# Where layer 0 puts the routing arithmetic and the projections of the next head pair

## The chip, the cores and the metric

The kernel runs on one core of one Trainium2 chip. The metric is the device time of one execution in microseconds; the times shown are medians of several runs. The profile shows one execution, engine by engine: TensorE (PE, with PEld for its weight loads), VectorE (DVE), ScalarE (ACT), GpSimd (POOL) and SyncE (SP).

## The reference, cut to what matters

The input `x` has eight images of 256 channels and 32 x 32 places, taken as 1024 tokens of 256. Layer 0 is attention with 8 heads of 64; its softmax runs over the queries (axis 1 of `i, j`), not over the keys:

```python
qkv = (xt @ w_qkv + b_qkv).reshape(B, S, N_HEADS, 3 * D_K)
attn = jnp.einsum('bihd,bjhd->bijh', q, k) * SCALE
attn = jax.nn.softmax(attn, axis=1)
res = jnp.einsum('bijh,bjhd->bihd', attn, v).reshape(B, S, N_HEADS * D_K)
res = res @ w_out + b_out + xt
```

Layer 1 normalises the tokens and adds a one-head attention over them; then it normalises again and adds a mixture of eight experts, of which each token uses two:

```python
logits = tokens @ router_w.T
probs = jax.nn.softmax(logits, axis=-1)
rw, re = jax.lax.top_k(probs, TOP_K)
rw = rw / jnp.maximum(rw.sum(-1, keepdims=True), 1e-12)
out = out + combine[:, e:e + 1] * y      # y: expert e's two-layer network
```

Everything is in float32.

## The kernel before, in words

The images are worked on one after another. For each image come layer 0 (`layer0`, line 370), the attention of layer 1 (`attend`, line 549) and the normalisation with the router's logits (`normed`, line 715). Seven images then send their normalised tokens to a table in HBM, sorted by expert; the experts run over that table afterwards, and the eighth image goes through the experts without sorting.

Layer 0 goes through the 8 heads in 4 pairs. A pair `g` has 8 steps `j`, one for each block of 128 keys, so a step is named (g, j) here, and `at` counts the 32 steps through. In a step both heads of the pair get their scores `psc` (line 395), as matmuls on 64 x 64 quarters of TensorE; a head's 1024 scores per key lie in a PSUM buffer called `big`, of which there are three. VectorE takes the maximum of the first half (`first_max`, line 410) and of the second half (line 422); ScalarE takes the exponential of the whole and its sum (line 432), which frees the buffer. VectorE turns the sum into its reciprocal and scales the values with it (`divide`, lines 441 and 443). Two steps later (`LAG = 2`) the value products `po` (`gather_values`, line 463) use the exponentials, in two turns of four matmuls. They add up over the 8 steps of a pair in two PSUM buffers; after the pair's last step ScalarE copies both to `res` (line 482), and only then can the next pair's products begin in the same buffers. Products that write the same half are kept apart by an empty instruction on SP (on POOL for image 0), which each turn waits for (line 471).

The queries and keys of pair g + 1 are made while pair g runs: `project` (line 294) is four matmuls of 128 x 512 into one more `big` buffer (line 300) and two evictions by VectorE (line 290). In the kernel before, the queries are projected in step (g, 3) and the keys in (g, 5), for g = 0, 1, 2.

The routing of the image before is fed into the layer 0 of the image after it. `dispatch` (line 728) and `gates` (line 641) are generators: each `yield` ends a portion, and layer 0 runs one portion in each step (lines 509 and 520). A portion is a few operations on 128 x 64 or 128 x 8 elements on VectorE, placed by `issue_after` behind the step's second first-half maximum. The portions are: softmax over the experts, the best and the second-best expert, their gates, two small matmuls `pcn` that count tokens before this one (lines 743 and 744), a running sum, the row of the table for each token and choice, and then 16 scatters on POOL, each preceded by a cast of its row numbers to integers on VectorE (line 795) and each one indirect DMA (line 797). Image 0 has no routing beside it.

The order in which an engine executes is fixed when the program is built: a scheduler places the instructions of each engine in the order of the program text, its priorities (`issue_after` among them) and the buffers, so matmuls of neighbouring calls can stand interleaved.

Of the kernel before, what the change touches and what calls it, by code (L numbers as in the profile page):

```python
# [11 lines left out]
I32 = mybir.dt.int32  # L12
# [7 lines left out]
def kernel(  # L20
# [349 lines left out]
    def layer0(b, xT, begun, routing):  # L370
# [8 lines left out]
        res = one.tile([P, NPAIR, S], F32, tag="res", name=f"res_{b}")  # L379
        steps = [(g, j) for g in range(NPAIR) for j in range(NT)]  # L380
        LAG = 2
        seconds, turned = {}, {}

        relay = nc.gpsimd if b == 0 else nc.sync
# [98 lines left out]
            return mm  # L483

        last = len(steps) - 1
        for at in range(last + LAG + 1):
            if at <= last:
                score(at, 0, 0)
            if 0 < at <= last + 1:
                score(at - 1, 1, 1)  # L490
                soften(at - 1, 1)
            if at >= LAG:
                gather_values(at - LAG, 0)
            if at <= last:
# [12 lines left out]
            if at == 0:  # L507
                begun.rest()
                next(routing, None)
            if at >= LAG:  # L510
                array = gather_values(at - LAG, 1)
            if at <= last:
                g, j = steps[at]
                if g + 1 < NPAIR and j in (3, 5):
                    if j == 3:
                        qks.append([])
                    qks[g + 1].append(project(b, xT, g + 1, len(qks[g + 1])))
                if array is not None:
                    with tc.issue_after(firsts[at, 1].ins), tc.issue_after(array.ins):
                        next(routing, None)  # L520
        for _ in routing:
            pass

# [117 lines left out]
    def gates(b, lT):  # L641


        def tmp(tag):
            return small.tile([P, NT, E], F32, tag=tag, name=f"{tag}_{b}", bufs=1)

        def col(tag):
            return small.tile([P, NT], F32, tag=tag, name=f"{tag}_{b}", bufs=1)

        n = S // NG  # L650
        pt = acc(f"plT_{b}")
        for j in range(n // P):
            nc.tensor.transpose(pt[:, ts(j, P)], lT[:, ts(j, P)], ident)

        l = tmp("g_l")
        nc.vector.tensor_copy(
            l.rearrange("p (g j) e -> p j g e", g=NG),
            pt[:, :n].rearrange("p (j g e) -> p j g e", g=NG, e=GC)[:, :, :, :E],
        )
        yield  # L660
        m = col("g_m")
        nc.vector.tensor_reduce(m, l, AX.X, ALU.max)
        p = tmp("g_p")
        nc.vector.tensor_sub(p, l, bcast(m, E))
        nc.scalar.activation(p, p, AF.Exp)
        yield
        z = col("g_z")
        nc.vector.tensor_reduce(z, p, AX.X, ALU.add)
        nc.vector.reciprocal(z, z)
        nc.vector.tensor_mul(p, p, bcast(z, E))  # L670
        yield

        def first_of_max(src, tag):
            top, best = col(f"{tag}_top"), col(f"{tag}_best")
            hot = tmp(f"{tag}_hot")
            nc.vector.tensor_reduce(top, src, AX.X, ALU.max)
            nc.vector.tensor_tensor(hot, src, bcast(top, E), ALU.is_equal)
            yield
            nc.vector.tensor_mul(hot, hot, rank)
            nc.vector.tensor_reduce(best, hot, AX.X, ALU.max)  # L680
            nc.vector.tensor_tensor(hot, hot, bcast(best, E), ALU.is_equal)
            return top, hot

        top1, hot1 = yield from first_of_max(p, "g_1")
        yield
        rest = tmp("g_rest")
        nc.vector.scalar_tensor_tensor(rest, hot1, -2.0, p, ALU.mult, ALU.add)
        top2, hot2 = yield from first_of_max(rest, "g_2")
        yield
        total = col("g_total")  # L690
        nc.vector.tensor_add(total, top1, top2)
        nc.vector.tensor_scalar_max(total, total, 1e-12)
        nc.vector.reciprocal(total, total)
        gate = keep.tile([P, 2, NT], F32, tag="gate", name=f"gate_{b}")
        nc.vector.tensor_mul(gate[:, 0], top1, total)
        nc.vector.tensor_mul(gate[:, 1], top2, total)
        return gate, (hot1, hot2)
# [30 lines left out]
    def dispatch(b, n2, l, group):  # L728

        gate, hots = yield from gates(b, l)  # L730
        yield

        def tmp(tag):
            return small.tile([P, NT, E], F32, tag=tag, name=f"{tag}_{b}", bufs=1)


        both = tmp("d_both")
        nc.vector.tensor_add(both, hots[0], hots[1])
        yield
# [7 lines left out]
        yield  # L747
# [11 lines left out]
        yield  # L759
# [12 lines left out]

        kept = []
        tos = []
        for k in range(2):
            yield
# [8 lines left out]
            yield  # L785
            to = small.tile([P, NT], F32, tag="d_to", name=f"d_to_{b}_{k}", bufs=2)
            nc.vector.scalar_tensor_tensor(to, exp, float(group.cap), row, ALU.mult, ALU.add)
            kept.append((row, exp))
            tos.append(to)
            group.kept[b] = gate, kept  # L790

        for k in range(2):
            for i in range(NT):
                at = small.tile([P, 1], I32, tag="d_at", name=f"d_at_{b}_{i}_{k}", bufs=4)
                nc.vector.tensor_copy(at, tos[k][:, i : i + 1])  # L795
                view = group.views[2 * (NT * group.items.index(b) + i) + k]
                nc.gpsimd.indirect_dma_start(  # L797
                    out=view[:, :],
                    out_offset=bass.IndirectOffsetOnAxis(ap=at, axis=0),
                    in_=n2[:, i, :],  # L800
                    in_offset=None,
                )
                yield

    def plan(group):

# [371 lines left out]
    begun = Begin(0, next_x)  # L1178
    begun.all()
    prepare()  # L1180
    routing = iter(())
    for b in range(B):
        xT = next_x
        if b + 1 < B:
# [65 lines left out]
```

## Time and profile before

| | |
|---|---|
| median of 3 runs | 2530.41 us (2528.81 to 2532.02) |
| profiled execution | 2521.92 us |
| its span in the profile | 2520.2 us |
| TensorE busy | 2421.3 us (96%) |
| VectorE busy | 1565.1 us (62%) |
| ScalarE busy | 887.7 us (35%) |
| GpSimd busy | 386.4 us (15%) |
| layer 0 of image 2, from 549.05 to 687.50 us | 138.45 us: TensorE busy 133.90, VectorE 112.54, ScalarE 77.45 |

In a line of the timeline the first number is the start in us from the span's beginning, the second the duration; then follow the engine, the line of the kernel, the operation, the tiles written and read, and how many instructions were merged. A bracket at the end gives the idle time of the engine just before and what ended it. One matmul of the kernel shows as two instructions[...]; hence groups of eight for four matmuls. Busy times of TensorE are modelled and overlap where quarters of the array run beside each other.

### The profile page before, as it was taken

The numbers are of one execution on the slowest core, as the hardware profiler recorded it, in microseconds if no ns is written. First come the engines' busy times: TensorE is split into PE (matmuls) and PEld (weight loads), VectorE is DVE, ScalarE is ACT, GpSimd is POOL, SyncE is SP. The second block draws the span as 40 slices with busy tenths as digits, with TensorE's granted clock in tenths as the row PEclk, the third lists the DMA queues.
The fourth block names the chain that finished last, engine by engine and source line by source line (L and its number), as shares of the span: only waits on it lengthen the run. The fifth ranks groups of instructions, "written<-read, shape, count | busy, mean of one in ns | idle before, by whom it ended". The sixth has DMA issues, their size and how long they took to land.

```text
span 2520.2 us, 37152 instructions
## 1 busy us (share of the span) xinstructions
PE 2421.3 (96%) x14015; PEld 1334.8 (53%) x14015; DVE 1565.1 (62%) x3836; ACT 887.7 (35%) x1491; POOL 386.4 (15%) x383
## 2 busy tenths in 40 slices
PE   9999999999999999999999999999999999997799
PEld 3356434653465346533663356335633688875466
DVE  5774677468755884578557855875578643334443
ACT  2541355125512561246225521552154422211222
POOL 0000002000200020002000100010001344434452
PEclk9999999999999999999999999999999999998899
DMA  7992001000100000000000000000001266653353
GB/s 281 385 361 69 34 3 44 6 17 1 35 17 17 1 30 21 17 1 28 24 17 1 25 27 17 1 22 14 1 18 49 91 214 213 217 186 101 98 162 119
DMA packets 82556, 188.23 MB, mean 75 GB/s; under 512 B 13992, under 2 KB 23880, under 8 KB 80584
## 3 DMA queue, kind: packets, MB, share of 16 engines
q1 hardware_dynamic: 57368, 118.65, 13.1%
q0 software_dynamic: 25008, 67.20, 8.6%
q8 instruction: 111, 1.82, 0.3%
q14 instruction: 69, 0.57, 0.1%
HBM read 100.49 MB, written 110.90 MB: 84 GB/s over the span
## 4 chain that ended last, share of the span: by engine, by line
PE 72%; DVE 9%; ACT 3%; issue 2%; DMA 1%; another core or an unknown queue 1%; ACTq 0%; DVEq 0%; SPq 0%; POOLq 0%
PE po L463 13%; PE psc L395 12%; PE pqk L300 8%; PE py L602 7%; PE ps L576 6%; PE pr L542 4%; PE ph L937 4%; PE pe L962 3%; PE pv L336 3%; DVE scrap L422 3%; PE pdy L1144 2%; PE pdh L1120 2%; PE px L561 2%; PE pa L595 2%; ACT ex L432 2%
## 5 line engine op out<-in xcount | busy, mean ns | idle before, releaser
L432 ACT ACTIVATE ex<-psc,nmax 128x1024 f32<-128x1024 f32 x512 | 571.1, 1115 | 528.2 <-DVE scrap L422 408.9
L463 PE MATMUL po<-ex,vs 64*64 64x512 f32 x4096 | 612.8, 593 | 25.4 <-ACT res L482 21.3
L395 PE MATMUL psc<-qk,qk 64*64 64x512 f32 x4096 | 613.4, 596 | 17.3 <-ACT ex L432 16.3
L422 DVE TENSOR_SCALAR_CACHE_REDUCE scrap<-psc,nmax 128x512 f32<-128x512 f32 x512 | 383.9, 750 | 118.3 <-PE psc L395 98.7
L410 DVE TENSOR_REDUCE nmax<-psc 128x1 f32<-128x512 f32 x512 | 350.5, 684 | 11.9 <-PE psc L395 11.9
L395 PEld LDWEIGHTS psc<-qk,qk 64*64 64x64 f32 x4096 | 188.0, 132 | 320.7 <-issue 167.8
L463 PEld LDWEIGHTS po<-ex,vs 64*64 64x64 f32 x4096 | 187.2, 132 | 285.0 <-issue 91.3
L602 PE MATMUL py<-n,aT 128*128 128x256 f32 x1024 | 243.5, 392 | 19.3 <-DVE aT L597 14.5
L797 POOL DMA_INDIRECT rows<-n,d_at x112 | 109.3, 976 | 926.1 <-DVE d_at L795 919.7
L602 PEld LDWEIGHTS py<-n,aT 128*128 128x128 f32 x1024 | 195.4, 195 | 84.2 <-DVE aT L597 52.3
L576 PE MATMUL ps<-nT,xa 128*128 128x512 f32 x512 | 236.5, 592 | 0.0
L300 PE MATMUL pqk<-xT,wqkv 128*128 128x512 f32 x512 | 235.0, 602 | 0.1
L587 ACT ACTIVATE ex<-ps,nmax 128x1024 f32<-128x1024 f32 x64 | 71.3, 1115 | 353.7 <-DVE nmax L584 338.5
L607 DVE SCALAR_TENSOR_TENSOR t<-py,rs,t 128x256 f32<-128x256 f32 x64 | 31.0, 484 | 234.3 <-PE py L602 202.3
L723 POOL TENSOR_TENSOR t<-t,n 128x2048 f32<-128x2048 f32 x8 | 36.3, 4533 | 901.6 <-issue 631.3
L300 PEld LDWEIGHTS pqk<-xT,wqkv 128*128 128x128 f32 x512 | 93.3, 190 | 133.0 <-issue 92.8
L576 PEld LDWEIGHTS ps<-nT,xa 128*128 128x128 f32 x512 | 93.6, 190 | 79.9 <-issue 73.6
L1009 POOL DMA_INDIRECT yk<-y,yat x112 | 112.6, 1006 | 122.4 <-DVE o L1041 71.5
L290 DVE TENSOR_SCALAR qk<-pqk,b_qk 128x512 f32<-128x512 f32 x100 | 75.1, 751 | 85.1 <-PE pqk L300 85.1
L336 PE MATMUL pv<-wqkv,xT 128*128 128x512 f32 x256 | 119.6, 597 | 0.8 <-ACT wqkv L106 0.8
L584 DVE TENSOR_REDUCE nmax<-ps 128x1 f32<-128x1024 f32 x64 | 78.3, 1223 | 59.1 <-PE ps L576 58.6
L542 PE MATMUL pr<-wo,res 128*128 128x256 f32 x512 | 111.8, 379 | 0.0
(191 smaller groups left out, 2441.4 us busy)
## 6 DMA issues: line engine op xcount, KB each, us to landing
rows<-wb SPq DMA_DIRECT2D x7, 8192.0 KB
y<-yb SPq DMA_DIRECT2D x63, 256.0 KB
xT<-in_x_dram SPq DMA_DIRECT2D x7, 1024.0 KB
sums<-t SPq DMA_DIRECT2D x7, 1024.0 KB
o<-sums SPq DMA_DIRECT2D x7, 1024.0 KB
out_dram<-oT SPq DMA_DIRECT2D x14, 512.0 KB
wpack<-in_L_ffn_w_dram SPq DMA_DIRECT2D x4, 1024.0 KB
wb<-in_L_ffn_w_dram SPq DMA_DIRECT2D x16, 256.0 KB
```

What stands on the lines that cost most here:

```text
L300: mm = nc.tensor.matmul(pq[:, ts(n, 512)], wqkv[:, cc, t, ts(g, P)], xT[:, cc, ts(n, 512)], start=(cc == 0), stop=(cc == NCC - 1),)
L336: nc.tensor.matmul(pv, self.xT[:, cc, ts(i, P)], wqkv[:, cc, 2, :], start=(cc == 0), stop=(cc == NCC - 1),)
L395: mm = nc.tensor.matmul(pss[at, h][ts(c, DK), ts(n, 512)], k[r, j * P + c * DK : j * P + (c + 1) * DK], q[r, ts(n, 512)], start=True, stop ...
L410: firsts[at, h] = nc.vector.tensor_reduce(nmax, pss[at, h][:, ts(0, 512)], AX.X, ALU.max, negate=True)
L422: seconds[h] = nc.vector.tensor_scalar(scrap, ps[:, ts(1, 512)], -1.0, nmaxes.pop((at, h)), ALU.mult, ALU.min, accum_out=nmax,)
L432: nc.scalar.activation(ex, ps, AF.Exp, bias=nmax, scale=1.0, accum_out=sums[at][:, h : h + 1])
L463: mm = nc.tensor.matmul(po[n][ts(h, DK), :], vss[at][keys, h, :], exps[at, h][keys, ts(n, 512)], start=(j == 0 and turn == 0), stop=(j == ...
L542: nc.tensor.matmul(pr[:, :C], res[:, g, ts(i, P)], wo[:, g, :], start=(g == 0), stop=(g == NPAIR - 1))
L576: nc.tensor.matmul(psc[:, ts(n, 512)], xa[:, ec, ts(i, P)], nT[:, ec, ts(n, 512)], start=(ec == 0), stop=(ec == NCC - 1),)
L602: nc.tensor.matmul(py[:, :D], aT[:, ts(m, P)], n1[:, m, :], start=(m == 0), stop=(m == NT - 1))
L797: nc.gpsimd.indirect_dma_start(out=view[:, :], out_offset=bass.IndirectOffsetOnAxis(ap=at, axis=0), in_=n2[:, i, :], in_offset=None,)
L1009: nc.gpsimd.indirect_dma_start(out=yk[:, i, k, :], out_offset=None, in_=self.group.y[:, :], in_offset=bass.IndirectOffsetOnAxis(ap=ats[k][ ...
```

## The change

Three things move, and one operation is merged; what is computed stays the same.

The steps that project become (0, 3), (0, 5), (1, 1), (1, 5), (2, 1), (2, 5). In step (g, 1) the value products of the pair before end, so there the projection now stands directly behind them.

The routing has fewer `yield`s. Its arithmetic runs in step (0, 0) and beside the first four projections, each portion placed before the projection; the scatters follow from (1, 6) on, one per step. Each scatter gets a dependency on the step's second first-half maximum (`behind`), passed in with `send`. The row numbers are cast once for each choice, 8 columns at a time, in place of once for each scatter.

Where a pair's first value products have no projection in front of them (only in step (3, 2)), their first turn is moved behind the step's remaining scores (`late`).

```diff
+        PROJECT = [(0, 3), (0, 5)]
+        PROJECT += [(g, j) for g in range(1, NPAIR - 1) for j in (1, 5)]
+        FIRST_SCATTER = PROJECT[3]
...
+        def share(behind=None):
+
+            try:
+                routing.send(behind)
+            except StopIteration:
+                pass
+
         for at in range(last + LAG + 1):
+            g, j = steps[min(at, last)]
+
+            late = at > LAG and steps[at - LAG][1] == 0 and (g, j - 1) not in PROJECT
             if at <= last:
                 score(at, 0, 0)
             if 0 < at <= last + 1:
                 score(at - 1, 1, 1)
                 soften(at - 1, 1)
-            if at >= LAG:
+            if at >= LAG and not late:
                 gather_values(at - LAG, 0)
...
             if at == 0:
                 begun.rest()
-                next(routing, None)
+                share()
+            if late:
+                gather_values(at - LAG, 0)
             if at >= LAG:
                 array = gather_values(at - LAG, 1)
-            if at <= last:
-                g, j = steps[at]
-                if g + 1 < NPAIR and j in (3, 5):
-                    if j == 3:
-                        qks.append([])
-                    qks[g + 1].append(project(b, xT, g + 1, len(qks[g + 1])))
-                if array is not None:
-                    with tc.issue_after(firsts[at, 1].ins), tc.issue_after(array.ins):
-                        next(routing, None)
+            project_now = at <= last and (g, j) in PROJECT
+            if at <= last and (project_now or (g, j) > FIRST_SCATTER):
+                with tc.issue_after(firsts[at, 1].ins), tc.issue_after(array.ins):
+                    share(firsts[at, 1])
+            if project_now:
+                if len(qks) == g + 1:
+                    qks.append([])
+                qks[g + 1].append(project(b, xT, g + 1, len(qks[g + 1])))
...
-            tos.append(to)
-            group.kept[b] = gate, kept
+            at = small.tile([P, NT], I32, tag=f"d_at{k}", name=f"d_at{k}_{b}", bufs=1)
+            nc.vector.tensor_copy(at, to)
+            ats.append(at)
+        group.kept[b] = gate, kept
 
         for k in range(2):
             for i in range(NT):
-                at = small.tile([P, 1], I32, tag="d_at", name=f"d_at_{b}_{i}_{k}", bufs=4)
-                nc.vector.tensor_copy(at, tos[k][:, i : i + 1])
+                behind = yield
                 view = group.views[2 * (NT * group.items.index(b) + i) + k]
-                nc.gpsimd.indirect_dma_start(
+                scatter = nc.gpsimd.indirect_dma_start(
                     out=view[:, :],
-                    out_offset=bass.IndirectOffsetOnAxis(ap=at, axis=0),
+                    out_offset=bass.IndirectOffsetOnAxis(ap=ats[k][:, i : i + 1], axis=0),
                     in_=n2[:, i, :],
                     in_offset=None,
                 )
-                yield
+                if behind is not None:
+                    tc.add_manual_dep(scatter.ins, behind.ins.name, BEHIND)
```

The rest of the diff removes `yield`s from `gates` and `dispatch` and turns `first_of_max` into a plain function.

More of the change, by code (lines that the diff above doesn't have):

```diff
@@ L670, in gates @@
         nc.vector.tensor_mul(p, p, bcast(z, E))
-        yield
         def first_of_max(src, tag):
@@ L677, in first_of_max @@
             nc.vector.tensor_tensor(hot, src, bcast(top, E), ALU.is_equal)
-            yield
             nc.vector.tensor_mul(hot, hot, rank)
@@ L682, in first_of_max @@
             return top, hot
-        top1, hot1 = yield from first_of_max(p, "g_1")
-        yield
+        top1, hot1 = first_of_max(p, "g_1")
         rest = tmp("g_rest")
         nc.vector.scalar_tensor_tensor(rest, hot1, -2.0, p, ALU.mult, ALU.add)
-        top2, hot2 = yield from first_of_max(rest, "g_2")
         yield
+        top2, hot2 = first_of_max(rest, "g_2")
         total = col("g_total")
@@ L730, in dispatch @@
         gate, hots = yield from gates(b, l)
-        yield
         def tmp(tag):
@@ L738, in dispatch @@
         nc.vector.tensor_add(both, hots[0], hots[1])
-        yield
         yield
@@ L746, in dispatch @@
         nc.vector.tensor_copy(cn.rearrange("p t i e -> p (t i e)"), pcn[:, : 2 * NT * E])
-        yield
         per = small.tile([P, E, NT], F32, tag="d_per", name=f"d_per_{b}", bufs=1)
@@ L758, in dispatch @@
         )
-        yield
         rows = tmp("d_rows")
@@ L773, in dispatch @@
         kept = []
-        tos = []
+        ats = []
+        yield
         for k in range(2):
-            yield
             hot = hots[k]
@@ L784, in dispatch @@
             nc.vector.tensor_reduce(exp, sel, AX.X, ALU.add)
-            yield
             to = small.tile([P, NT], F32, tag="d_to", name=f"d_to_{b}_{k}", bufs=2)
@@ L802, in dispatch @@
                 )
-                yield
+                if behind is not None:
+                    tc.add_manual_dep(scatter.ins, behind.ins.name, BEHIND)
     def plan(group):
@@ L1180 @@
     prepare()
-    routing = iter(())
+    routing = (nothing(_) for _ in ())
     for b in range(B):
```

## The prediction

> **What bounds the kernel.** I read the page first: TensorE is the path.
>
> ```profile
> span 2520.2 us, 37152 instructions
> ...
> PE 2421.3 (96%) x14015; PEld 1334.8 (53%) x14015; DVE 1565.1 (62%) x3836; ACT 887.7 (35%) x1491; POOL 386.4 (15%) x383
> ...
> PE 72%; DVE 9%; ACT 3%; issue 2%; DMA 1%; another core or an unknown queue 1%; ACTq 0%; DVEq 0%; SPq 0%; POOLq 0%
> ```
>
> So only what keeps TensorE waiting or thinly fed in layer 0, the stage the change touches, can be won. Next, the timeline of image 2, one undisturbed step (start, duration, what):
>
> ```profile
> 682.79 1.22 PE L395 MATMUL psc<-qk,qk 64*64 64x512 f32 x8
> 683.00 1.11 ACT L432 ACTIVATE ex<-psc,nmax 128x1024 f32<-128x1024 f32 x1 [0.32 <-DVE rs L441]
> 683.65 1.22 PE L463 MATMUL po<-ex,vs 64*64 64x512 f32 x8
> 684.01 0.19 ACT L432 ACTIVATION_READ_ACCUMULATOR ex<-psc,nmax 128x1 f32 x1
> ...
> 684.51 1.22 PE L395 MATMUL psc<-qk,qk 64*64 64x512 f32 x8
> ...
> 685.37 1.22 PE L463 MATMUL po<-ex,vs 64*64 64x512 f32 x8
> ```
>
> Four groups of eight follow each other every 0.86 us: a full step is 3.43 us, and VectorE waits for TensorE in it. This is the floor. A pair's switch is not at it:
>
> ```profile
> 665.51 1.06 ACT L482 COPY res<-po 128x512 f32<-128x512 f32 x2
> ...
> 666.14 1.14 PE L463 MATMUL po<-ex,vs 64*64 64x512 f32 x6 [0.90 <-ACT res L482]
> ...
> 668.12 0.75 DVE L422 TENSOR_SCALAR_CACHE_REDUCE scrap<-psc,nmax 128x512 f32<-128x512 f32 x1 [1.32 <-PE psc L395]
> ```
>
> The new pair's value products wait for the copies that free `po`; the scores behind them wait too, so VectorE idles. A step that projects (line 300), last:
>
> ```profile
> 559.34 3.70 PE L300 MATMUL pqk<-xT,wqkv 128*128 128x512 f32 x8
> ...
> 559.78 0.68 DVE L410 TENSOR_REDUCE nmax<-psc 128x1 f32<-128x512 f32 x1
> ...
> 560.38 0.21 DVE L668 TENSOR_REDUCE g_z<-g_p 128x8 f32<-128x64 f32 x1
> ...
> 563.08 0.75 DVE L290 TENSOR_SCALAR qk<-pqk,b_qk 128x512 f32<-128x512 f32 x1 [0.97 <-PE pqk L300]
> ...
> 564.13 0.75 DVE L422 TENSOR_SCALAR_CACHE_REDUCE scrap<-psc,nmax 128x512 f32<-128x512 f32 x1 [0.30 <-PE psc L395]
> ...
> 566.00 0.19 ACT L432 ACTIVATION_READ_ACCUMULATOR ex<-psc,nmax 128x1 f32 x1
> ...
> 566.46 1.04 PE L395 MATMUL psc<-qk,qk 64*64 64x512 f32 x8
> ```
>
> Here VectorE has a hole: between its maximum (done 560.46) and the next reduction (564.13) lie 3.67 us, of which two evictions need 1.50. Cover: 2.17 us.
>
> As a clock I take the starts of line 441's reciprocal, one per step. Plain steps give 3.43, projecting ones 7.23. Pair sums (8, 8, 8 and 7 gaps): image 0, which has no routing, 35.01, 36.67, 36.65, 25.51; image 2, which has it, 36.33, 38.87, 36.66, 25.36. Images 3 to 6 equal image 2 within 0.2. Images 1 and 7 have 6.3 and 5.6 more in one pair (image 1's value products are issued late; the blocks are planned in image 7's), in an order the change leaves alone.
>
> [...] ready scores stand behind the 0.90 us wait. [...] a projection among the 64x64 groups takes 3.63 us on the chain, in the attention part 3.43. [...] 64 elements take 225 ns (line 670), 504 take 676 (line 838), so the 39 small routing operations are nearly all fixed cost. [...] 24 waits for `po`'s two buffers, 21.3 us.
>
> **A, the pair switch (8 images).** In image 0, pair 1 starts 4.58, 3.68, 7.45 where 3.43, 3.43, 7.23 would be plain: 1.62 lost; pair 2: 1.61; pair 3: 4.57, 3.69, 3.47, 1.44 lost. For pairs 1 and 2 the projection now stands behind the last values: 3.63 us of matmuls cover the copies (they end at 666.57, 2.4 us after the last values' group at 664.20), and ScalarE has 4.2 us of idle in a projecting step, so the exponential that the copies delay today is not late. The evictions move with the projection (twice 0.75 us, the same hole in VectorE's row), and the `qk` buffer that they write had its last reader, the scores of the pair before, one step earlier. The whole 3.23 goes; were the projection not long enough, up to 1.6 per switch would come back. For pair 3 eight scores are moved ahead of the first value products. Half of them need the PSUM buffer of the current step's first exponential, whose accumulator read ends 1.41 us after the last values, so they finish about 2.0 after; the copies end at 1.9 to 2.4. Then 16 value products (1.72) and a relay wait (0.1 to 0.3, the trace's end of layer 0) give a step of 3.9 to 4.2, so 0.5 to 0.75 stays; I take 0.70, saving 0.74. Sum 3.97 x 8 = **31.8 us**.
>
> **B, routing out of plain steps (7 images).** A step with three or four small operations becomes VectorE-bound (3.8 to 4.05 us). Image 2 less image 0: pair 0 1.32, pair 1 2.20 (0.91 of it the step that also holds the `pcn` products). 3.52 x 7 = **24.6 us**. The 98 saved casts (143 ns) count nothing: VectorE waited 0.16 us per step even with them.
>
> **C, what comes back (7 images).** The built order puts 9, 11, 7 and 12 small operations into (0,3), (0,5), (1,1), (1,5), ahead of the evictions or among them. Dependent ones start 0.25 us apart (617.00, 617.25, 617.50), the 8-wide ones 0.18: 2.25, 2.4, 1.7, 2.75 us against 2.17. Overrun 0.1, 0.25, none, 0.6. Behind them stand the evictions, then the second head's reduction and exponential, for whose PSUM TensorE's scores wait; slack there is 566.46 - 566.19 = 0.27. Stall: 0, 0, 0, 0.3. In (0,0) two more operations stand before a reduction with 0.45 us of wait: nothing.
> In (1,1) `pcn` now stands *before* the projection and takes the buffer freed by the previous exponential; the projection gets the next one, freed by the current step's first exponential, 1.41 us after the last values plus 0.06 to 0.4 of signalling, where a plain projection starts after 0.14. Stall 1.33 to 1.67, `pcn`'s 0.6 inside; I take 1.5. TensorE's other work queues behind it. (1.5 + 0.3) x 7 = **12.6 us**.
> The 16 scatters, one indirect DMA of 0.97 us on POOL each, move from pair 2's second step to the end of layer 0 into (1,6) to (3,5), behind a maximum each: POOL is idle there; they end earlier, each holding only later scatters and the next image's addition (line 723) behind it, and what waits for them (next normalisation, the experts' gathers) waits no longer than now. SP's queue is unchanged.
>
> Sum: 31.8 + 24.6 - 12.6 = 43.8. The profiled execution took 2521.92 us (span 2520.2): 2478.1; the median of the runs is 2530.41, 0.34% higher, so **2486 us**.
>
> **Rivals.**
> 1. Crowding takes a good part back (2504): small operations at 0.35 us. Then 9, 11 and 12 of them take 3.15, 3.85 and 4.2 us, less cover and slack of 2.44: stalls of 0.7, 1.4 and 1.8 where I have 0.3, so 3.6 x 7 = 25 at most; the eight-wide ones are shorter, I take 18. A stall of 4 us in (1,1) gives the same. For it: three steps already exceed the cover. Against: the 0.25 us is measured in this very queue.
> 2. Stalls only move (2530, within 5): what follows a switch is then bound by ScalarE or VectorE. Against: steady steps show VectorE waiting for TensorE (0.16 us), ScalarE at 0.7 idle.
> 3. Slower (2541): one mechanism, VectorE's queue in steps (0,3), (0,5), (1,5). Their 32 small operations must cost the 43.8 / 7 = 6.3 us gained per image and 0.2 of slack left over: 32 x (s - 0.25) > 6.5, so it decides from a spacing s of 0.45 us; at 0.5 it gives 32 x 0.25 - 0.2 = 7.8 per image, 2541. For it: these operations stand ahead of everything that feeds the next step. Nothing in the trace shows above 0.26.
> That the order is not as described is excluded by the instruction order of both builds.
>
> **Numbers.** Forecast 0.77, rival 1 0.15, rival 2 0.05, rival 3 0.03. Own range of the forecast 2477 to 2496 (pair 3 saving 0 to 1.2, (1,1) 1.3 to 2.5, switches 2.6 to 3.3 per image); with rival 1, 2477 to 2510. A measurement of this kernel tells about 0.2% (5 us) from no change: faster 0.93, same 0.04, slower 0.03.
>
> **What would show it.** A right: no wait of `po` for `res` left but about 8 short ones at pair 3; pair 1 and 2 start with 3.43-like gaps. B right: images 2 to 6 pair 0 at 35.0, VectorE's steps free of small operations. C right: a wait of `pqk` for `ex`, about 1 us, seven times, and pair 1 at 36.8 against image 0's 35.0. Wrong if small operations run slower beside evictions, if POOL's or SP's relays delay the products put back to back in pair 3, or if a fuller TensorE is granted a lower clock.

## The result and the profile after

The changed kernel takes 2485.19 us (median, 2483.84 to 2486.23), the kernel before 2530.69 beside it: a ratio of 0.982, 95% interval 0.9803 to 0.9837. The forecast was 2486. The profiled execution took 2485.58 us, 36.3 less than that of before.

First the page's summary lines, the answer to those of before:

```profile
span 2483.9 us, 37112 instructions
...
PE 2405.0 (97%) x14015; PEld 1310.7 (53%) x14015; DVE 1564.7 (63%) x3738; ACT 888.4 (36%) x1491; POOL 388.6 (16%) x383
...
PE 78%; DVE 4%; ACT 2%; issue 1%; another core or an unknown queue 1%; DMA 1%; ACTq 0%; POOL 0%; DVEq 0%; SPq 0%; POOLq 0%
```

VectorE's busy time is nearly the same (1565.1 before) although 98 instructions are gone, yet its part of the chain that ends last fell from 9% to 4% and TensorE's rose from 72% to 78%: the work was hardly made less, it was moved off the path. Next three of the page's costliest groups, before and after (us busy, mean ns of one, then the idle us of the engine ahead of them and what ended most of it):

```profile
L463 PE MATMUL po<-ex,vs 64*64 64x512 f32 x4096 | 612.8, 593 | 25.4 <-ACT res L482 21.3
L395 PE MATMUL psc<-qk,qk 64*64 64x512 f32 x4096 | 613.4, 596 | 17.3 <-ACT ex L432 16.3
...
L300 PE MATMUL pqk<-xT,wqkv 128*128 128x512 f32 x512 | 235.0, 602 | 0.1
```


```profile
L399 PE MATMUL psc<-qk,qk 64*64 64x512 f32 x4096 | 568.2, 593 | 7.3 <-ACT ex L436 7.2
L467 PE MATMUL po<-ex,vs 64*64 64x512 f32 x4096 | 558.4, 591 | 5.4 <-DVE vs L447 4.1
...
L300 PE MATMUL pqk<-xT,wqkv 128*128 128x512 f32 x512 | 235.0, 602 | 5.4 <-ACT ex L436 5.2
```

The wait of `po` for `res` is gone as a group (21.3 us before), and a new wait of `pqk` for `ex`, 5.2 us, has come. Those are two of the three signs that the prediction named.

The clock of the prediction, the starts of the reciprocal (now line 445), gives the third. Sums in us for image 2, and what the prediction's parts give for the same pair:

| pair | before | after | saved | forecast |
|---|---|---|---|---|
| 0 | 36.33 | 35.08 | 1.25 | 1.32 |
| 1 | 38.87 | 36.41 | 2.46 | 1.62 + 2.20 - 1.5 - 0.3 = 2.02 |
| 2 | 36.66 | 35.05 | 1.61 | 1.61 |
| 3 | 25.36 | 24.98 | 0.38 | 0.74 |
| all | 137.22 | 131.52 | 5.70 | 5.69 |

Over the eight images these sums went from 1106.57 to 1062.38 us: 44.2 saved, 43.8 forecast. Image by image the two lie further apart: image 0 saved 3.57 of 3.97, images 1 to 6 saved 5.42 to 5.83 of 5.69, and image 7 saved 6.76, since its pair 2, beside which the experts' blocks are planned, went from 42.28 to 39.34, 2.94 less where 1.61 was forecast. Behind the last image's layer 0, where the change does nothing, the profiled execution of before took 541.7 us and that of after 549.7; so the two profiled executions differ by 36.3 us only, where the medians differ by 45.5.

Now the three places, from the timeline of image 2 (start, duration, what). The switch to pair 2:

```profile
613.30 1.04 PE L467 MATMUL po<-ex,vs 64*64 64x512 f32 x8
...
614.27 3.70 PE L300 MATMUL pqk<-xT,wqkv 128*128 128x512 f32 x8
...
615.47 1.06 ACT L486 COPY res<-po 128x512 f32<-128x512 f32 x2
...
617.90 1.09 PE L399 MATMUL psc<-qk,qk 64*64 64x512 f32 x8
...
618.81 1.04 PE L467 MATMUL po<-ex,vs 64*64 64x512 f32 x8
```

The copies end at 616.53, 2.3 us before the new pair's value products want `po`. No product waits for them. A step that projects and carries nine routing operations:

```profile
550.01 0.68 DVE L414 TENSOR_REDUCE nmax<-psc 128x1 f32<-128x512 f32 x1
550.61 0.21 DVE L682 TENSOR_REDUCE g_z<-g_p 128x8 f32<-128x64 f32 x1
550.86 0.20 DVE L683 RECIPROCAL g_z<-g_z 128x8 f32<-128x8 f32 x1
...
552.63 0.22 DVE L698 SCALAR_TENSOR_TENSOR g_rest<-g_hot,g_p 128x64 f32<-128x64 f32 x1
552.78 1.40 DVE L290 TENSOR_SCALAR qk<-pqk,b_qk 128x512 f32<-128x512 f32 x2
554.46 0.75 DVE L426 TENSOR_SCALAR_CACHE_REDUCE scrap<-psc,nmax 128x512 f32<-128x512 f32 x1 [0.28 <-PE psc L399]
```

VectorE still waits 0.28 us for TensorE at the end: the hole holds them. And the second step of pair 1, where time comes back:

```profile
577.86 0.43 PE L752 MATMUL pcn<-d_both,before 128*128 128x64 f32 x2
577.96 1.11 ACT L436 ACTIVATE ex<-psc,nmax 128x1024 f32<-128x1024 f32 x1 [0.34 <-DVE rs L445]
...
578.97 0.19 ACT L436 ACTIVATION_READ_ACCUMULATOR ex<-psc,nmax 128x1 f32 x1
...
579.22 3.70 PE L300 MATMUL pqk<-xT,wqkv 128*128 128x512 f32 x8 [0.70 <-ACT ex L436]
```

The small `pcn` takes the free PSUM buffer, and the projection has to wait for the exponential that starts only now: the step takes 8.58 us instead of 7.23, 1.35 more.

### The profile page after: what moved, and what is told of

The parts are those of the page before. It is cut to its first block, busy times and chain, and to the rows that moved or that the text cites. A ratio compares the mean times of both kernels' runs of the same rounds, so it can differ in the third digit from the quotient of the medians.

```text
span 2483.9 us, 37112 instructions
## 1 busy us (share of the span) xinstructions
PE 2405.0 (97%) x14015; PEld 1310.7 (53%) x14015; DVE 1564.7 (63%) x3738; ACT 888.4 (36%) x1491; POOL 388.6 (16%) x383
## 4 chain that ended last, share of the span: by engine, by line
PE 78%; DVE 4%; ACT 2%; issue 1%; another core or an unknown queue 1%; DMA 1%; ACTq 0%; POOL 0%; DVEq 0%; SPq 0%; POOLq 0%
PE psc L399 15%; PE po L467 15%; PE py L617 8%; PE pqk L300 8%; PE ps L591 6%; PE ph L945 4%; PE pr L557 4%; PE pe L970 4%; PE pv L336 3%; PE pdy L1152 2%; PE px L576 2%; PE pdh L1128 2%; PE pa L610 2%; ACT ex L436 1%
## 5 line engine op out<-in xcount | busy, mean ns | idle before, releaser
L399 PE MATMUL psc<-qk,qk 64*64 64x512 f32 x4096 | 568.2, 593 | 7.3 <-ACT ex L436 7.2
L467 PE MATMUL po<-ex,vs 64*64 64x512 f32 x4096 | 558.4, 591 | 5.4 <-DVE vs L447 4.1
L399 PEld LDWEIGHTS psc<-qk,qk 64*64 64x64 f32 x4096 | 174.8, 132 | 299.5 <-issue 148.9
L467 PEld LDWEIGHTS po<-ex,vs 64*64 64x64 f32 x4096 | 166.7, 132 | 285.1 <-issue 97.6
```

Source lines behind the costliest of these rows:

```text
L399: mm = nc.tensor.matmul(pss[at, h][ts(c, DK), ts(n, 512)], k[r, j * P + c * DK : j * P + (c + 1) * DK], q[r, ts(n, 512)], start=True, stop ...
L467: mm = nc.tensor.matmul(po[n][ts(h, DK), :], vss[at][keys, h, :], exps[at, h][keys, ts(n, 512)], start=(j == 0 and turn == 0), stop=(j == ...
```

## The experiments

Three theories were to be told apart. The prediction's: waits at the switch go, routing hides beside the projection, a PSUM buffer brings 1.5 us back per image. Rival: what is gained at a switch or by moving the routing depends on the other part, or only moves. Rival: crowding on VectorE is the limit. The runs were made in batches, on several chips; between batches, also between two that bear the same chip number, the part behind layer 0 differs by up to 38 us while layer 0's steps agree to some hundredths, so each run is read by its ratio to the kernel before beside it and by its own layer-0 gaps, and never by its bare time against a run made elsewhere. "Layer-0 sum" is the sum of the table above over the eight images.

### The changed kernel once more

> The changed kernel unchanged, beside the kernel before on another chip, as the base for the experiments. Ratio to the kernel before 0.982 again; its image-by-image times in layer 0 equal to 0.1 us to those of its first trace; what lies behind layer 0 (549.7 us in its first trace, 541.7 in that of the kernel before) differs with the granted clock, since the change does nothing there.

Measured: 2477.68 against 2522.35 us, ratio 0.9819 (0.9805 to 0.9832). The layer-0 sum is 1062.97 (1062.38 in the first trace), the pairs of image 2 are 35.08, 36.40, 35.05 and 24.98. Behind the last layer 0 it took 539.4 us, ten less than in the first trace of the very same kernel. So a difference of 8 us in that part, as between the two traces shown above (541.7 us at a granted clock of 0.96 and 549.7 at 0.95), comes up without any change to the kernel. Image 7's pair 2 took 39.92 here and 39.34 in the first trace, so that pair too varies by itself.

### Each part alone

The projections alone, put into the kernel before:

```diff
+        PROJECT = [(0, 3), (0, 5)]
+        PROJECT += [(g, j) for g in range(1, NPAIR - 1) for j in (1, 5)]
...
-                if g + 1 < NPAIR and j in (3, 5):
-                    if j == 3:
+                if (g, j) in PROJECT:
+                    if len(qks) == g + 1:
```

with the line for `late` as in the change.

> The kernel before, with only the projections put behind a pair's last values and pair 3's eight scores put ahead of its first value products; the routing's portions stay as they were, one per step. Theory: the switch is a part by itself. Pair 2 goes from 36.66 to 35.05 us in every image, pair 3 from 25.36 to 24.98, image 0's pair 1 from 36.67 to 35.05; pair 0 of images 2 to 6 stays at 36.3, and pair 1 goes from 38.87 to about 37.2 (its switch gone, its routing still there). Saved: 8 x (1.61 + 1.62 + 0.37) = 28.8 us, to about 2502. Rival (the two parts need each other, because routing operations ahead of the moved evictions delay the next pair's scores): less than 20 us saved, with pair 1 above 38 us. Rival (stalls only move): pair 1 and pair 2 keep their sums within 0.3 us.

Measured: 2466.42 against 2493.3 us, ratio 0.989 (0.9874 to 0.9905); layer-0 sum 1079.23, 27.3 less than before. Pair 2 is at 34.93, pair 3 at 24.98, pair 0 stays at 36.34. Pair 1 comes to 37.75, not 37.2. The gaps show where the half microsecond is: the projections have left the third step, so the `pcn` products now stand in a plain step, which takes 4.96 us, 1.53 more than 3.43; in the kernel before they stood behind a projection and cost 0.91. TensorE's timeline of this kernel:

```profile
592.73 0.43 PE L748 MATMUL pcn<-d_both,before 128*128 128x64 f32 x2
593.00 0.39 PE L749 MATMUL pcn<-d_both,ones 128*128 128x64 f32 x2
594.09 1.09 PE L397 MATMUL psc<-qk,qk 64*64 64x512 f32 x8 [0.70 <-ACT ex L434]
```

The scores wait 0.70 us for the exponential, as the projection does in the changed kernel.

The routing alone:

```diff
-        PROJECT = [(0, 3), (0, 5)]
-        PROJECT += [(g, j) for g in range(1, NPAIR - 1) for j in (1, 5)]
+        PROJECT = [(g, j) for g in range(NPAIR - 1) for j in (3, 5)]
...
-            late = at > LAG and steps[at - LAG][1] == 0 and (g, j - 1) not in PROJECT
+            late = False
```

> The changed kernel, with the projections back in the third and fifth step of pairs 0 to 2, and pair 3's order as before; the routing's portions stand in those projecting steps, all else in the routing is as changed. Theory: the switches' stalls come back, pair 1 +1.6, pair 2 +1.6, pair 3 +0.37 per image, so the time is 8 x 3.6 = 29 us above the changed kernel, about 2514, and 16 below the kernel before. Pair 0 of images 2 to 6 is at 35.1 us, since routing is out of its plain steps; pair 1 near 38.0 (36.4 + 1.6). Rival (the gain of pair 0 comes from where its projections stand, not from the routing): pair 0 at 36.3.

Measured: 2476.11 against 2493.3 us, ratio 0.9933 (0.9919 to 0.9946); layer-0 sum 1089.30, 17.3 less than before. Pair 0 of image 2 is at 35.08 and pair 1 at 37.83 with the switch's gaps back (4.57, 3.72). Pair 0's gain is the routing's, its projections stand where they stood. The merged casts are in this part too; no share of theirs shows, since in the kernel before steps with one cast and one scatter took 3.43 us as well (the fourth to sixth of image 2's pair 3).

The two parts, 27.3 and 17.3, add up to 44.6 us where the whole change gave 44.2. They don't need each other, and the stalls didn't move elsewhere.

### Pair 3's order undone

```diff
-            late = at > LAG and steps[at - LAG][1] == 0 and (g, j - 1) not in PROJECT
+            late = False
```

> The changed kernel, with one part undone: at pair 3's start the first half of its first value products stands ahead of the eight scores again, as before; all else stays. Theory (as the trace of the changed kernel shows it, 0.36 to 0.38 us saved per image at pair 3): pair 3's seven gaps go back from 24.98 to 25.35 us (image 0: 25.15 to 25.5), the other pairs stay; the time rises by 8 x 0.37 = 3 us, to about 2488. The prediction's step (0.74 saved per image) would give 8 x 0.74 = 6 us, 2491. Rival (stalls only move): no change within 1 us, since pair 3's start is bound by the copies in either order.

Measured: ratio 0.9835 (0.9822 to 0.9849); pair 3 at 25.35 to 25.36 (image 0 25.51), the other pairs unchanged but for image 7's pair 2 (41.04). The order is worth 0.37 us per image, half of the 0.74 forecast.

### Where the pcn products stand

```diff
-    def project(b, xT, g, t, scalar=False):
+    def project(b, xT, g, t, scalar=False, between=None):
...
             evicted[b, g, t] = evict(dst[:, ts(n, 512)], pq[:, ts(n, 512)], g, t, scalar)
+            if n == 0 and between is not None:
+                between()
...
-            if at <= last and (project_now or (g, j) > FIRST_SCATTER):
+            count_now = project_now and (g, j) == PROJECT[2]
+            if at <= last and (project_now or (g, j) > FIRST_SCATTER) and not count_now:
...
-                qks[g + 1].append(project(b, xT, g + 1, len(qks[g + 1])))
+                between = (lambda: share(firsts[at, 1])) if count_now else None
+                qks[g + 1].append(project(b, xT, g + 1, len(qks[g + 1]), between=between))
```

> The changed kernel, with one thing moved: in the second step of pair 1 the portion with the pcn products is issued between the two halves of the projection, not ahead of both. So the projection's first half takes the PSUM buffer that the last exponential of the step before freed, and pcn the one that the current step's first exponential frees, under the cover of the projection's 1.7 us. Theory (the 1.35 us that this step of images 1 to 7 takes over 7.23 are the projection's wait for its PSUM buffer): the step's gap goes from 8.58 to about 7.7 (pcn's own 0.2 us and one wait of at most 0.3 stay), pair 1 from 36.41 to about 35.5, so 7 x 0.85 = 6 us less: about 2479. Rival (the 1.35 us are the small operations ahead of the evictions on VectorE, and the buffer is only named by the trace): the gap stays at 8.4 or more, the time at 2485. Rival (the operations between the two evictions delay the second one and so the scores): the gap grows beyond 8.6.

Measured: 2442.45 against 2493.3 us, ratio 0.9797 (0.9783 to 0.9810). The step takes 7.67 us (8.58), pair 1 35.50 (36.41), the layer-0 sum is 1055.74: 6.6 us below the changed kernel's first trace and 7.2 below its second. The same place in this kernel's timeline:

```profile
576.84 1.98 PE L300 MATMUL pqk<-xT,wqkv 128*128 128x512 f32 x4
...
578.66 0.33 PE L756 MATMUL pcn<-d_both,before 128*128 128x64 f32 x2
...
579.05 1.94 PE L300 MATMUL pqk<-xT,wqkv 128*128 128x512 f32 x4
...
580.91 1.09 PE L401 MATMUL psc<-qk,qk 64*64 64x512 f32 x8
```

The first half of the projection takes the free buffer, the exponential ends under it, and `pcn` finds its buffer free. The small operations ahead of the second eviction are the same in number; the wait was the buffer's. This is the version that beats both kernels in layer 0. Its ratio and that of the changed kernel (0.9819) were not taken side by side, and their intervals overlap, so the gain rests on the gaps of the traces.

### Filling VectorE's hole

```diff
                 with tc.issue_after(firsts[at, 1].ins), tc.issue_after(array.ins):
                     share(firsts[at, 1])
+                    if project_now:
+                        crowd(b, at, 8)
```

`crowd` writes a 128x64 tile (half of a part of `v`) and then halves it in place, 8 operations in all (16 in the second kernel), each on the one before; nothing reads it.

> The changed kernel plus 8 small dependent operations of VectorE (128x64, each on the one before) in each of the six projecting steps of every image, behind the routing's own and ahead of the evictions. By the prediction's cover (2.44 us, 0.25 us per operation): image 0 and pair 2, which have no routing there, 2.0 us, no stall (7.23); images 2 to 6: step (0,3) 17 operations, 1.8 us of stall, (0,5) 19, 2.0, (1,5) 20, 2.3, (1,1) about 0.3 behind its own wait: 6.4 per image, 45 us in all, so the gain over the kernel before is gone. If the cover is larger (step (1,5) showed no stall with 12, so at least 2.75 us): each of the three steps loses as much less. Rival (crowding, small operations slow down beside the evictions, 0.35 us apart): image 0's projecting steps are above 7.3 already, and the spacing is seen in the trace.

> As the kernel with 8, with 16 small operations per projecting step. By the prediction's cover of 2.44 us: image 0 and pair 2 have 4.0 us, 1.6 of stall per projecting step (7.23 to 8.8); images 2 to 6: (0,3) 3.8, (0,5) 4.0, (1,5) 4.3, (1,1) about 1.4, pair 2 twice 1.6: 16.7 per image, some 126 us in all. From 8 to 16 operations each step that is past its cover grows by 8 x 0.25 = 2.0 us; where it grows by less, the difference is cover left over at 8. Rival (crowding): the growth is 8 x 0.35 = 2.8 us.

With 8: ratio 0.9839 (0.9824 to 0.9854), layer-0 sum 1063.66, 0.7 above the unchanged kernel. In image 2 not one projecting step is longer: 7.22 or 7.23 with 8, 17, 19 and 20 operations, and 8.58 in (1,1) as without them. The stall of 6.4 us per image did not come. With 16: ratio 0.9995 (0.9987 to 1.0004), layer-0 sum 1106.92, 44 us more, a third of the 126 expected. VectorE's timeline of the kernel with 8 says why:

```profile
550.41 0.21 DVE L690 TENSOR_REDUCE g_z<-g_p 128x8 f32<-128x64 f32 x1
550.54 0.18 DVE L499 TENSOR_SCALAR crowd<-v 128x64 f32<-128x64 f32 x1
550.66 0.20 DVE L691 RECIPROCAL g_z<-g_z 128x8 f32<-128x8 f32 x1
550.78 0.18 DVE L501 TENSOR_SCALAR crowd<-crowd 128x64 f32<-128x64 f32 x1
...
552.44 0.23 DVE L706 SCALAR_TENSOR_TENSOR g_rest<-g_hot,g_p 128x64 f32<-128x64 f32 x1
552.59 1.40 DVE L290 TENSOR_SCALAR qk<-pqk,b_qk 128x512 f32<-128x512 f32 x2
554.27 0.75 DVE L426 TENSOR_SCALAR_CACHE_REDUCE scrap<-psc,nmax 128x512 f32<-128x512 f32 x1 [0.28 <-PE psc L399]
```

The scheduler laid the two chains into each other. The nine routing operations still start 0.25 us apart, and the eight others stand in between, so that each operation starts 0.11 to 0.15 us after the one of the other chain. From the first one to the evictions it is 2.18 us with seventeen operations, and it was 2.17 with nine. So about half of the 0.25 us from one link to the next is wait for its result, an estimate from these spacings; the eight operations of the second chain went into that wait for nothing.

The kernel with 16 tells where the hole ends, since now it is too small. The same step:

```profile
559.59 0.69 DVE L414 TENSOR_REDUCE nmax<-psc 128x1 f32<-128x512 f32 x1
...
562.37 0.88 DVE L501 TENSOR_SCALAR crowd<-crowd 128x64 f32<-128x64 f32 x4
563.16 0.75 DVE L290 TENSOR_SCALAR qk<-pqk,b_qk 128x512 f32<-128x512 f32 x1
563.82 0.87 DVE L501 TENSOR_SCALAR crowd<-crowd 128x64 f32<-128x64 f32 x4
564.61 0.74 DVE L290 TENSOR_SCALAR qk<-pqk,b_qk 128x512 f32<-128x512 f32 x1
565.27 0.74 DVE L426 TENSOR_SCALAR_CACHE_REDUCE scrap<-psc,nmax 128x512 f32<-128x512 f32 x1
```

From the maximum's end (560.28) to the second reduction (565.27) it is 4.99 us, and the step takes 8.23, 1.00 more than 7.23. So 3.99 would have cost nothing. In step (0,5) it is 5.39 with 1.41 lost, hence 3.98; in image 0, 4.65 with 0.65, hence 4.00. The prediction had the hole at 3.67 plus 0.27 of slack, 3.94. The cover was right; the price of the operations put into it was wrong, since 0.25 us each holds for one chain alone. For rival 3 that means: a spacing of 0.45 us, which it needs, was not near in the changed kernel: in the three steps that it names none passed 0.26 in images 2 to 7 (image 1 has one of 0.33). Alone in their chain the added operations start 0.23 apart.

One slowing does show in both crowded kernels. In pair 2's projecting steps of images 1 to 7 a scatter runs on POOL beside the added operations; each time three of them that it overlaps take 0.20 us as elsewhere, and the fourth takes 0.42 and ends with the scatter (14 times in each kernel). In step (2,1) of image 2, with 16:

```profile
628.77 0.97 POOL L812 DMA_INDIRECT rows<-n,d_at  x1 [2.46 <-DVE crowd L499]
...
629.32 0.42 DVE L501 TENSOR_SCALAR crowd<-crowd 128x64 f32<-128x64 f32 x1
```

With 16 this step takes 8.11 us, and the same step of image 0, which has no scatter, 7.89. So the small VectorE operations beside a scatter were not free here; that it is the scatter that holds the operation is read from the equal ends, no run moved it. In the changed kernel these steps have no small operations.

### What is left at pair 3's start

The second step of pair 3 takes 4.47 us where 3.43 is plain. In the changed kernel's timeline:

```profile
649.21 2.12 PE L399 MATMUL psc<-qk,qk 64*64 64x512 f32 x14
...
650.67 0.19 PEld L399 LDWEIGHTS psc<-qk,qk 64*64 64x64 f32 x4 [0.47 <-ACT ex L436]
...
651.63 0.19 PEld L467 LDWEIGHTS po<-ex,vs 64*64 64x64 f32 x4 [0.29 <-ACT res L486]
...
652.34 0.68 PEld L467 LDWEIGHTS po<-ex,vs 64*64 64x64 f32 x8 [0.51 <-SPq L477]
...
653.40 1.35 PE L399 MATMUL psc<-qk,qk 64*64 64x512 f32 x8
...
656.94 0.37 PEld L399 LDWEIGHTS psc<-qk,qk 64*64 64x64 f32 x8 [0.49 <-ACT ex L436]
656.96 1.23 PE L399 MATMUL psc<-qk,qk 64*64 64x512 f32 x8
...
660.53 1.10 PE L399 MATMUL psc<-qk,qk 64*64 64x512 f32 x8
...
664.01 1.05 PE L399 MATMUL psc<-qk,qk 64*64 64x512 f32 x8
```

Three waits stand in a row: the scores' second group for the first exponential, the value products for the copies, the second turn for the relay through SyncE (the empty instruction that keeps two turns apart).

Plain products start every 0.107 us (32 in 3.43); counted so, TensorE has lost 0.18 us at the first of these waits, 0.29 at the second and 0.77 behind the third. The step that holds them takes 4.19 us (649.21 to 653.40), and the three behind it 3.56, 3.57 and 3.48, which loses 0.30 more: 1.07 in all. In the kernel before the same count gives 1.20 at the switch and 0.23 behind it, 1.43.

Five kernels, all built on the one with `pcn` between the projection's halves, took them on. The second copy on VectorE:

```diff
                 for n in range(NH2):
-                    nc.scalar.copy(res[:, g, ts(n, 512)], po[n])
+                    if n == 1 and g == NPAIR - 2:
+                        nc.vector.tensor_copy(res[:, g, ts(n, 512)], po[n])
+                    else:
+                        nc.scalar.copy(res[:, g, ts(n, 512)], po[n])
```

> The kernel with the pcn portion between the projection's halves, and one more thing: of the two copies that free po at the end of pair 2, the second is made by VectorE instead of ScalarE. It is there to see what the second step of pair 3 still waits for (4.47 where 3.43 is plain). Theory: the copies are in series on ScalarE (done 2.4 us after the last values' group), so with the second one beside the first the second half of the value products starts 0.5 us earlier: gap 4.47 to about 4.1, 8 x 0.35 = 3 us. Rival: the scores' second group, whose PSUM buffer the current step's first exponential frees, and the relayed second turn set the step: the gap stays at 4.4 to 4.5. Rival: the copy (0.75 us) on VectorE delays the second maximum and the exponential behind it: the gap grows, to 4.8 or so.

Measured: ratio 0.9798 (0.9784 to 0.9811); the gaps 3.48 and 4.47 become 3.75 and 4.09, pair 3 goes to 24.88, 0.10 less. What the values gain, the second maximum and its exponential lose.

The second turn's halves in the other order:

```diff
-            for half in range(2):
+            for half in (1, 0) if swap else (0, 1):
...
-                array = gather_values(at - LAG, 1)
+                array = gather_values(at - LAG, 1, swap=late)
```

> The kernel with the pcn portion between the projection's halves, and one thing more: where the two turns of pair 3's first value products stand back to back, the second turn takes its two halves in the other order, so that its first group follows the relay sent after the first turn's first half (two groups earlier) and not the one sent just before. Theory (the relay through SyncE, 0.51 us in the trace, is one of the terms that set the step of 4.47 us): the step goes to about 4.1, pair 3 from 24.98 to 24.6, 8 x 0.4 = 3 us in all. Rival (the copies and the first exponential set it, and the relay only fills time that is lost anyway): pair 3 stays at 24.9 or above.

Measured: ratio 0.9822 (0.9803 to 0.9841); pair 3 stays at 24.98, the wait of 0.51 us stays too. So the edit didn't take the relay out of the way, and the run says nothing of what the relay costs; why the wait stayed is not shown.

The copies left out:

```diff
+        nc.gpsimd.memset(res[:, NPAIR - 2, :], 0.0)
...
                 for n in range(NH2):
-                    nc.scalar.copy(res[:, g, ts(n, 512)], po[n])
+                    if g != NPAIR - 2:
+                        nc.scalar.copy(res[:, g, ts(n, 512)], po[n])
```

> The kernel with the pcn portion between the projection's halves, with pair 2's two copies out of po left out (its part of res is set to zero on GpSimd at the start of the image; so the values of pair 2 are missing from the output). It prices all that the copies cost at pair 3's start. Prediction's step (the copies, ended 1.9 to 2.4 us after the last values, and the scores' second half, about 2.0 after, end together): without the copies the step still waits for the first exponential and the relay, so it goes from 4.47 only to about 4.1, pair 3 to 24.6. Rival (the copies alone): 3.43 to 3.6, pair 3 at 24.1 or below.

Measured: 2473.12 us, one execution. Pair 3 is at 24.88, its second gap at 4.48. With no copy at all, this gap is as long as with both; the one before it falls from 3.48 to 3.37. Its timeline:

```profile
647.01 2.11 PE L402 MATMUL psc<-qk,qk 64*64 64x512 f32 x14
...
648.48 0.20 PEld L402 LDWEIGHTS psc<-qk,qk 64*64 64x64 f32 x4 [0.47 <-ACT ex L439]
...
649.86 0.13 PEld L470 LDWEIGHTS po<-ex,vs 64*64 64x64 f32 x1 [0.34 <-SPq L480]
...
651.10 1.35 PE L402 MATMUL psc<-qk,qk 64*64 64x512 f32 x8
```

Both other waits stand there still, and TensorE's step is 4.09 us long (4.19 in the changed kernel).

Halves and copy together, and then the copy with the first turn put between the two groups of four scores, so that the relay passes under the second group:

> Both of these together, with the output complete: the second turn's halves in the other order, and pair 2's second copy on VectorE. If relay and copies are in series, both gains add (0.10 measured for the copy, 0.4 for the relay): pair 3 at 24.5, 4 us below the kernel with the pcn portion between the halves alone. If either is hidden by the other or by the first exponential, pair 3 stays within 0.1 of the better of the two.

> The kernel with the pcn portion between the projection's halves and pair 2's second copy on VectorE; in addition the first turn of pair 3's first value products stands between the two groups of four scores of that step, not behind both, so that no two turns stand back to back and the relay passes under four scores. Theory (with the copies beside each other, what is left at pair 3 is the wait for the first exponential, 0.2 us, and the relay, 0.3 to 0.5): pair 3 goes from 24.88 to about 24.5 us, 8 x 0.35 = 3 us less. Rival (the later scores delay the second maximum and the exponentials behind it, which set the next step): pair 3 stays at 24.8 or grows.

```diff
                 score(at, 0, 1)
+                if late:
+                    gather_values(at - LAG, 0)
                 score(at, 1, 0)
...
-            if late:
-                gather_values(at - LAG, 0)
```

Measured: ratios 0.9825 (0.9810 to 0.9841) and 0.9799 (0.9786 to 0.9813); pair 3 at 24.88 and 24.87. Neither adds anything to the copy's 0.10. In the last one the value products stand earlier in the queue and wait for the copy instead (0.77 us). The ratios near 0.982 of the two kernels with the swapped halves are not a loss in layer 0: its sums are 1056.41 and 1056.72; they ran in a batch in which the part behind it took 551 us in both, without the changed kernel beside them.

So the copies are worth 0.10 us of the 1.07 that stay, shown by leaving them out. No edit took more than 0.11 us off pair 3: where one wait went, another stood in its place. The largest single loss is the one at the relay (0.48 us), but no run took it away alone, so what it is worth by itself is open.

## Why the prediction was right, and where it was not

**What bounds the kernel, and A for pairs 1 and 2: right.** 1.61 of 1.61 at pair 2, and the switch's gaps back with the projections at their old places. The 3.63 us of matmuls cover the copies, and the exponential behind the copies is not late.

**A, pair 3: right in its sign, half its size.** The step that failed is "give a step of 3.9 to 4.2, so 0.5 to 0.75 stays; I take 0.70". The loss of 1.44 before was read rightly, for every image (4.57, 3.69 and 3.47 in image 2 as well), and the step itself came out at 4.19, at the edge of the bounds. But the sum ends with that step, and 0.30 us more is lost in the steps behind it, which it put at nothing: 1.07 stay, and by the reciprocals' gaps (3.48, 4.47, 3.43) 1.09. Inside the step the terms were off too: the prediction took it from the copies and the scores ending together and gave the relay 0.1 to 0.3; leaving the copies out moved pair 3 by 0.10, and at the relay 0.48 is lost. (The 2.4 us to the end of the copies are rightly counted from 664.20, but that is where the scores behind the last values start; the values' own group starts at 663.34.)

**B: right.** 1.25 of 1.32 at pair 0, and the run with the routing alone gives it without any moved projection.

**C, the buffer in (1,1): right in place and cause.** 1.35 us where 1.5 was taken; the bracket was 1.33 to 1.67. With `pcn` between the halves the step loses 0.44 (7.67 for 7.23).

**C, the overrun in (1,5): wrong.** "2.75 us against 2.17", 0.3 us of stall: there is none. From the maximum's end to the second reduction it is 3.78 us in the changed kernel (597.75 to 601.53), within the 3.99 that cost nothing. The twelve operations take 2.40 us there and not 2.75, because they are two chains, one per choice, that the scheduler interleaves in part. The failed step is that it took the spacing of a dependent chain for the price of an operation. It also took the operations for nearly all fixed cost; by its own two durations (225 ns for 64 elements, 676 for 504) some 160 of the 225 ns are fixed, an estimate from these two. In the runs an operation that reads its forerunner's result starts 0.22 to 0.26 us after it, and one that doesn't 0.11 to 0.15.

**The sum.** Pair 1 gave 0.44 us more per image than forecast (0.15 from the buffer, 0.3 from the overrun), pair 3 gave 0.36 less. Two errors of opposite sign made 5.70 out of 5.69 in image 2; the total is better than its parts. Over the eight images there is a third: image 7, whose extra time the prediction left alone, gave 1.07 more than its share, and the other seven together 0.7 less than theirs.

**The rivals.** Crowding (rival 1) is excluded by the kernel with 8 more operations, stalls that only move (rival 2) by the two parts adding up, the slower case (rival 3) by spacings that never passed 0.26 us in the three steps it names (images 2 to 7). The scatters cost nothing that shows: pairs 1 to 3 have plain gaps of 3.43 with them in.

**From the profiled sum to the time.** The factor 2530.41 / 2521.92 was needed. The sum for the profiled execution, 2478.1, fell 7.5 us short of the 2485.58 measured, since the part behind layer 0 took 8.0 us more in that execution; against the medians the forecast is within a microsecond. That this part varies so much was not seen beforehand, so the closeness of the two is in part luck.

## What to carry to other kernels

Price a wait by the stage it stands in and by what stands next: here a whole projection (3.63 us of matmuls) was a cover long enough for both the copies and the routing, and only the work with no such cover (pair 3) kept most of its loss. Before putting a small extra product into a rotation of PSUM buffers, follow which release each later tile then waits for: the step that holds `pcn` took 1.53 us more in a plain step, 0.91 behind a projection, 1.35 ahead of one and 0.44 between its halves. Of these only the last two differ by the place alone; the other two kernels divide the routing differently. For small VectorE operations count chains, not operations: here one chain took 0.25 us at every link, and the eight operations of a second one fitted between its nine.

## What the runs showed of the hardware

- VectorE, 128x64 in 32 bits: a dependent operation starts 0.22 to 0.26 us after the one before it, an independent one 0.11 to 0.15; seventeen operations in two chains took 2.18 us, nine in one 2.17.
- A 128x64 operation of VectorE in the second half of an indirect DMA's 0.97 us on POOL took 0.42 us instead of 0.20 and ended with it, 28 times out of 28 in the two crowded kernels; three in the first half took 0.20.
- Layer 0's steps take the same time in every batch (3.43 and 7.23 to 0.01 us; the stretch between two images' layer 0 is 119.4 to 119.5), with a granted clock of 1.00 from 40 us to the last layer 0 in all fourteen traces. The part behind it took 512.6 to 515.0 us in five traces, with a clock of 0.97 to 0.98 there, and 539.4 to 551.0 in the nine others, with 0.94 to 0.96. Two batches on the same chip number fall on either side, so the difference isn't shown to be one of chips, and the part is 4.7 to 7.5% longer at a clock 1 to 4% lower, so it isn't shown to be all the clock.
- Two turns of value products put back to back leave TensorE's weight load 0.51 us of wait for the empty instruction on SyncE that orders them; with eight scores in between it is 0.28, as much as in front of loads that wait for nothing that shows.
